# Re-dealing the first microseconds of a three-stage transformer kernel, with identity products on an idle tensor engine and an earlier load of the output weights

## The chip, the cores and the metric

The kernel runs on one core of a Trainium2 chip. The metric is the device time of one execution in microseconds (us); the smaller the better. The profile is one execution, whose span runs from the first to the last instruction.

## The reference, cut to what matters

Three residual blocks follow each other on `x` (16 batches of 64 tokens, 512 channels), with a context of 16 x 512 x 512:

```python
x = x + xattn(ctx_1024, layernorm(x), mask, ...)   # latents attend to the context and themselves
x = x + attn(layernorm(x), Wq, Wk, Wv, Wo, ...)    # differential self-attention over 64 tokens
x = x + ffn(layernorm(x), w_gate, w_up, w_down)    # SwiGLU, weights and activations in blockwise FP4

# inside xattn:
ln = _ln(latents, g_l, b_l)
q = ln @ w_q
k, v = split(concat([_ln(ctx), ln]) @ w_kv)
out = softmax(q k^T * scale, masked) @ v
return _ln(out @ w_out, g_o, b_o)
```

The change touches the first block only, and the rate at which FP4 weights for the third are prepared beside it.

## The kernel before, in words

Every product in high precision is made of three products of rounded halves: a matrix is split into a high part (a copy in fp32r, by `high`) and a low part (the rest, by `low`), and `Common.terms` (L114) runs high*high, high*low and low*high over the four chunks `k` of 128 channels. It is a generator that yields after each of the three terms.

**The opening** is `_latents` (L455). `load`, `weight` and `cw.load` issue DMAs on the one SyncE queue, in the order of the program: two tiles of x, four small vectors (`vec_rows`), four chunks of w_k, four of w_q, one of w_v. `raw` has nine buffers, so the other chunks of w_v wait until chunks of w_k are used up. `moments` (L493) makes the mean on VectorE and the inverse deviation on GpSimd (`tensor_scalar` L499, `pow` L500); `norm` (L502) normalises on VectorE; `turn` (L506) transposes a tile on TensorE and applies gain and bias on the way out of PSUM (ScalarE, L520, for tile 0; VectorE, L518, for tile 1); `upper` and `lower` split the result; `cw.turn` (L392) transposes the small vectors into `vec`, and its last line (L399) subtracts one bias from another on GpSimd. Then `heads` (L593) makes k and q of two tiles (`lk`, `lq`) and `values` (L634) makes v (`lv`), for four groups of two tiles. Between products, `then` runs the side work that `during(n, ...)` had filed under slot n: splits of other weights, moments of the next tiles, bias sums. In the first k of group 0, three of the four output chunks go together, term by term (`late = 3`, L607), because the low parts come late. PSUM has three banks for `cm.mm`/`cm.tr`, one for `ps_av`, and two pairs for `cm.two`. `take` (L598) empties a bank on ScalarE.

**The loop over 16 batches** is `cross_attention` (L729). The engines run what they are given in program order, each at its own pace. A batch has four `keys` (`pk`), four `values` (`pv`), two `scores`, and the transposes and weighing (`turn_both`, `turn_latents`, `finish`) of the batch before; every odd batch from 3 on has an output projection (`out_product`) too. `keys` is emptied by a VectorE multiply (L810), `values` by ScalarE (L823). ScalarE also splits the coming context (`cx.high`) and casts, and `weight_o` (L974) splits the output weights w_out: high on ScalarE, low on GpSimd. `load_o` (L970) loads one chunk of w_out; two buffers under tag "o" hold all four chunks in turn, so chunks 0 and 1 are loaded and split late in batch 0, chunks 2 and 3 loaded at its end and split early in batch 1.

**The quantiser** (L241) is a stream of 35 pieces of FP4 weights. `tick` moves every active piece by one step, and starts a piece every fourth tick. Step 1 loads (SyncE), step 3 is the block maximum on VectorE (L194 to L197), step 4 is on GpSimd, 5 and 6 on VectorE and ScalarE (L202 to L208), 7 on GpSimd, 8 and 9 on VectorE and ScalarE (L287 to L290), step 10 stores. Batch 0 has three ticks, each later batch ten.

Of the kernel before, what the change touches and what calls it, by code (L numbers as in the profile page):

```python
# [9 lines left out]
F32 = mybir.dt.float32  # L10
# [35 lines left out]
def f32(t):  # L46

    return t.bitcast(F32)


class Common:
# [62 lines left out]
    def terms(self, ps, parts, ks, start=True, stop=True):  # L114

        terms = [(0, 2), (0, 3), (1, 2)]
        n, last = 0, len(terms) * len(ks) - 1
        for i, j in terms:
            for k in ks:
                p = parts(k)  # L120
                self.nc.tensor.matmul(  # L121
                    ps, lhsT=p[i], rhs=p[j], start=start and n == 0, stop=stop and n == last
                )
                n += 1
            yield

    def split(self, hi, lo, src, by=None):

# [242 lines left out]
class CrossWeights:  # L371
# [20 lines left out]
    def turn(self):  # L392
        cm, nc = self.cm, self.cm.nc
        n = len(self.NAMES) * KC
        pt = cm.tr("vec_t")[:, :n]
        nc.tensor.transpose(pt, self.rows, cm.ident[:n, :n])
        nc.scalar.copy(self.vec, pt)

        nc.gpsimd.tensor_tensor(self.bl, self.bl, self.bx, ALU.subtract)  # L399


class SelfConstants:
# [52 lines left out]
def _latents(ctx, tc, cm, sc, i, cw, cx, sa):  # L455
# [13 lines left out]
    def load(*tiles):  # L469
        for p in tiles:  # L470
            nc.sync.dma_start(cm.x[p], i["x"][p * P : (p + 1) * P, :])
# [3 lines left out]
            raws[name, k] = pool.tile([P, D], F32, tag="raw", bufs=9, name=f"raw_{name}_{k}")  # L475
            nc.sync.dma_start(raws[name, k], source[name][k * P : (k + 1) * P, :])

    def high(name, w, k):
        nc.scalar.copy(w[0][:, k, :], raws[name, k])

    def low(name, w, k, by=None):
        by = by or (nc.vector, nc.gpsimd)[k % 2]
# [7 lines left out]

    def moments(p):  # L493
        st = cm.small.tile([P, 6], F32, tag="st", name=f"st_l_{p}")
        mv = mvs[p] = cm.small.tile([P, 2], F32, tag="mv", name=f"mv_l_{p}")
        nc.vector.bn_stats(st, cm.x[p])
        nc.vector.bn_aggr(mv, st)
        r = mv[:, 1:2]
        nc.gpsimd.tensor_scalar(r, r, 1.0 + LN_EPS, LN_EPS * LN_EPS, ALU.mult, ALU.add)  # L499
        nc.gpsimd.tensor_tensor(r, r, cm.mhalf[:, :1], ALU.pow)  # L500

    def norm(p):  # L502
        zs[p] = pool.tile([P, D], F32, tag="lz", bufs=2, name=f"lz_{p}")
        cm.normalize(zs[p], cm.x[p], f"l_{p}", mvs.pop(p))

    def turn(p):  # L506
        g, n = divmod(p, GT)
        if n == 0:
            lns[g] = tuple(
                pool.tile([P, KC, GT * P], F32R, tag=f"ln{h}", bufs=2, name=f"ln{h}_{g}") for h in "hl"  # L510
            )
        pt = cm.tr(f"lt_{p}")
        cm.transpose_chunks(pt, zs.pop(p), KC)
        ln = pool.tile([P, KC, P], F32, tag="ln", bufs=2, name=f"ln_{p}")
        for k in range(KC):
            src, scale, bias = pt[:, k * P : (k + 1) * P], cw.gl[:, k : k + 1], cw.bl[:, k : k + 1]
            if p == 1:
                nc.vector.tensor_scalar(ln[:, k, :], src, scale, bias, ALU.mult, ALU.add)  # L518
            else:
                nc.scalar.activation(ln[:, k, :], src, AF.Identity, bias=bias, scale=scale)  # L520
        rows[p] = ln

    def upper(*tiles):
        for p in tiles:
            g, n = divmod(p, GT)
            nc.vector.tensor_copy(lns[g][0][:, :, n * P : (n + 1) * P], rows[p])

    def lower(*tiles):
        for p in tiles:
            g, n = divmod(p, GT)  # L530
            hi, lo = (t[:, :, n * P : (n + 1) * P] for t in lns[g])
            nc.vector.tensor_tensor(lo, rows.pop(p), f32(hi), ALU.subtract)

    def bias(name, k):

# [57 lines left out]
    def heads(g, what, w, dst, scale, bias=None):  # L593

        hi, lo = lns[g]
        st = pool.tile([P, KC, GT * P], F32, tag=f"{what}st", name=f"{what}st_{g}")

        def take(m, ps):  # L598
            if bias is None:
                nc.scalar.copy(st[:, m, :], ps)  # L600
            else:
                nc.scalar.activation(
                    st[:, m, :], ps, AF.Identity, bias=bias[:, m : m + 1], scale=scale
                )


        late = 3 if (g, what) == (0, "k") else 0  # L607
        lag = 2 if (g, what) == (0, "q") else 0
        made, ready = [], []
        for m in range(KC):  # L610
            cols = slice(m * P, (m + 1) * P)
            ps = cm.mm(f"l{what}_{g}_{m}")[:, : GT * P]
            terms = cm.terms(
                ps,
                lambda k, cols=cols: (w[0][:, k, cols], w[1][:, k, cols], hi[:, k, :], lo[:, k, :]),
                range(KC),
            )
            made.append((m, ps, terms))
            if m < late - 1:
                continue  # L620
            for _ in range(3):
                for _, _, steps in made:
                    next(steps)
            for _ in made:
                then()
            ready += made
            made = []
            while len(ready) > lag:
                take(*ready.pop(0)[:2])
        for at, done, _ in ready:  # L630
            take(at, done)
        nc.sync.dma_start(dst[g], st)

    def values(g):  # L634
        hi, lo = lns[g]
        for n, p in enumerate(groups[g]):
# [9 lines left out]
            nc.scalar.copy(vst, ps)  # L646
            nc.sync.dma_start(sc.v[p], vst)

    load(0, 1)
    cw.load(pool)  # L650
    weight("k", *range(KC))
    weight("q", *range(KC))
    weight("v", 0)
    load(2, 3)
    moments(0)
    cw.turn()
    norm(0)
    moments(1)
    norm(1)
    high("k", w_k, 0)  # L660
    turn(0)
    turn(1)
    for k in range(1, KC):
        high("k", w_k, k)
    upper(0, 1)
    lower(0, 1)
    for k in range(KC):
        low("k", w_k, k, nc.vector)
    for k in range(KC):
        high("q", w_q, k)  # L670
    for k in range(KC):
        low("q", w_q, k)
    weight("v", 1, 2, 3)
    load(4, 5, 6, 7)
    sa.load_norm(pool)
# [3 lines left out]
    during(5, bias_sum, "q", cw.bq, S**-0.5)  # L679
    during(16, sa.turn_norm)  # L680
    for k in range(KC):
        during(1 + k, high, "v", w_v, k)
        during(2 + k, low, "v", w_v, k)
        during(7 + k, bias, "v", k)
    during(12, bias_sum, "v", cw.bv, 1.0)
    for n in range(2, NT):
# [42 lines left out]
def cross_attention(tc, cm, sc, i, cw, cx, w1, w2, att, quant):  # L729
# [238 lines left out]
    raw_o = {}  # L968

    def load_o(k):  # L970
        raw_o[k] = w1.tile([P, D], F32, tag="o", bufs=2, name=f"raw_wo_{k}")
        nc.sync.dma_start(raw_o[k], i["w_out"][k * P : (k + 1) * P, :])

    def weight_o(k):  # L974
# [18 lines left out]
    for b in range(B):  # L993

        def tick():
            if b:
                quant.tick()

        done = (b - 3) // 2 if b >= 3 and b % 2 else None
        last = b == B - 1  # L1000
        keys(b, 0)
        if last:
            att.load("Wq")
            att.load("Wk")
        cx.high(b + 1, 0)
        if b >= 4 and b % 2 == 0:
            out_moments((b - 4) // 2)
        tick()
        keys(b, 1)
        if b == 1:  # L1010
            weight_o(2)
            weight_o(3)
        cx.low(b + 1, 0)
        cx.high(b + 1, 1)
        tick()
        if b:
            turn_both(b - 1)
            turn_latents(b - 1)
        if done is not None:
            out_turn(done)  # L1020
        keys(b, 2)
        cx.fetch(b + 2, 0)
        cx.flat(b + 1)
        cx.low(b + 1, 1)
        cx.high(b + 1, 2)
        tick()
        if last:
            att.split("Wq", 0, 1)
        if b:
            finish(b - 1)  # L1030
        tick()
        if last:
            att.split("Wq", 2)
        scores(b, 0)
        softmax(b, 0)
        around(b + 1, 2, 3)
        keys(b, 3)
        cx.fetch(b + 2, 1)
        cx.low(b + 1, 2)
        cx.high(b + 1, 3)  # L1040
        tick()
        values(b, 0)
        cx.every(b + 1)
        cx.low(b + 1, 3)
        cx.stats(b + 2, 0)
        tick()
        if last:
            att.split("Wq", 3)
            att.load("Wv")
        if b == 0:  # L1050
            load_o(0)
            load_o(1)
        values(b, 1)
        begin(b + 1)
        cx.fetch(b + 2, 2)
        cx.stats(b + 2, 1)
        tick()
        if last:
            att.norm(0)
            att.split("Wk", 0, 1)  # L1060
        turn(b, 0, 0)
        turn(b, 0, 1)
        scores(b, 1)
        softmax(b, 1)
        around(b + 2, 0, 1)
        if done is not None:
            out_product(done)
        quant.tick()
        values(b, 2)
        cx.fetch(b + 2, 3)  # L1070
        cx.stats(b + 2, 2)
        quant.tick()
        if done is not None:
            out_norm(done)
            out_add(done)
        if b == 0:
            weight_o(0)
            weight_o(1)
            load_o(2)
            load_o(3)  # L1080
        if b == 2:
            att.sa.load()
        if b == 5:
            att.sa.work()
        if last:
            att.split("Wk", 2, 3)
            att.load("Wo")
            att.turn(0)
        values(b, 3)
        cx.stats(b + 2, 3)  # L1090
        cx.spread(b + 2)
        mask(b + 1)
        quant.tick()
        cx.load(b + 3)
    turn_both(B - 1)
# [635 lines left out]
```

## Time and profile before

| what | value |
|---|---|
| median of three runs | 912.67 us |
| lowest of three runs | 911.80 us |
| the profiled execution, time | 912.59 us |
| its span | 910.7 us |
| PE busy | 886.9 us (97%) |
| DVE, ACT, POOL busy | 682.1, 399.9, 330.5 us |
| chain that ended last, share of PE | 85% |

PE is TensorE's matmul side and PEld its weight loads; DVE is VectorE, ACT ScalarE, POOL GpSimd, SP SyncE, with a "q" for a sequencer. A timeline row is: start, duration, engine, line, operation, output<-inputs, shape, xcount, and in brackets the idle time ahead of it and what ended that. The chain that ended last is followed back from the last instruction to what released each step. A waits row is: engine, line and what it waited for, us in total, times, longest.

### The profile page before, as it was taken

Reading aid. Unit: us, or ns where it says so; the run is one execution under the profiler, and the core shown is the slowest. Engines: PE = TensorE matmul, PEld = TensorE weight load, DVE = VectorE, ACT = ScalarE, POOL = GpSimd, SP = SyncE. Lnnn points to the kernel's source line nnn. Section 1 sums busy time; section 2 is a strip of 40 time slices with the busy share of each in tenths; the row PEclk is TensorE's granted clock in tenths of the full one; section 3 lists DMA queues with packets and bytes.
Section 4 is the critical chain, followed back from the end, with each engine's and each line's share of the span. In section 5 each row is a group of like instructions: output and inputs, shape, how many; then the busy total and the mean of one; then the engine's idle time right before and its main releaser. Section 6 shows DMA issues by size and latency. Waiting matters only on the chain.

```text
span 910.7 us, 17129 instructions
## 1 busy us (share of the span) xinstructions
PE 886.9 (97%) x6550; PEld 733.2 (81%) x6550; DVE 682.1 (75%) x1394; ACT 399.9 (44%) x782; POOL 330.5 (36%) x376
## 2 busy tenths in 40 slices
PE   5999999999999999999999999999999999999998
PEld 5898777878787887888778877778777788888886
DVE  7545467878799787786997964586878797888875
ACT  4464344544545444445444545545454423322221
POOL 5255153326254353263443621547564330100000
PEclk9999999999999999999999999999999999999999
DMA  7464565554555445345544452140005530000000
GB/s 241 176 242 138 152 187 166 152 178 146 150 161 150 159 157 174 112 138 151 161 147 144 133 149 102 47 185 2 2 1 212 229 139 12 12 12 12 13 13 24
DMA packets 80235, 111.11 MB, mean 122 GB/s; under 512 B 33161, under 2 KB 38809, under 8 KB 78873
## 3 DMA queue, kind: packets, MB, share of 16 engines
q1 hardware_dynamic: 79992, 109.48, 37.5%
q8 instruction: 52, 0.85, 0.4%
q0 software_dynamic: 160, 0.52, 0.2%
q14 instruction: 31, 0.25, 0.1%
HBM read 84.26 MB, written 25.72 MB: 121 GB/s over the span
## 4 chain that ended last, share of the span: by engine, by line
PE 85%; DVE 7%; ACT 3%; DMA 2%; issue 1%; SPq 1%; POOL 1%; ACTq 0%; DVEq 0%; POOLq 0%
PE pk L121 18%; PE pv L121 18%; PE gu L121 13%; PE dn L121 7%; PE av L904 4%; PE sim L836 4%; PE prt L171 3%; PE po L121 3%; PE Wv L121 2%; PE lv L121 2%; PE wo L121 2%; PE lq L121 2%; PE lk L121 2%; DVE ex L1266 1%; PE ht L171 1%; DMA raw_wo<-in_w_out_dram 1%
## 5 line engine op out<-in xcount | busy, mean ns | idle before, releaser
L121 PE MATMUL pv<-xvh,x 128*128 128x512 f32 x512 | 133.1, 392 | 0.0
L121 PE MATMUL pk<-x,xkh 128*128 128x512 f32 x512 | 130.5, 397 | 0.3 <-DVE k L810 0.3
L121 PEld LDWEIGHTS pk<-x,xkh 128*128 128x128 f32 x512 | 93.7, 188 | 26.0 <-issue 4.0
L121 PEld LDWEIGHTS pv<-xvh,x 128*128 128x128 f32 x512 | 95.3, 188 | 23.3 <-issue 2.2
L810 DVE TENSOR_TENSOR k<-pk,row 128x512 f32<-128x512 f32 x64 | 43.6, 683 | 47.0 <-PE pk L121 46.8
L823 ACT ACTIVATE v<-pv,rs 128x512 f32<-128x512 f32 x64 | 43.9, 686 | 79.4 <-PE pv L121 79.3
L859 ACT ACTIVATE pr<-pr,least 128x576 f32<-128x576 f32 x64 | 49.2, 772 | 55.1 <-DVE least L855 54.8
L368 POOL TENSOR_TENSOR x<-raw,x 128x512 fp32r<-128x512 f32 x32 | 44.2, 1382 | 78.0 <-ACT x L362 71.6
L121 PE MATMUL pk<-x,xkl 128*128 128x512 f32 x256 | 68.7, 390 | 0.0
L121 PE MATMUL pv<-xvl,x 128*128 128x512 f32 x256 | 68.5, 389 | 0.0
L121 PE MATMUL gu<-uT,fx 128*128 128x512 f32 (+1 forms) x288 | 67.8, 378 | 0.0
L121 PE MATMUL gu<-gT,fx 128*128 128x512 f32 (+1 forms) x288 | 65.5, 375 | 0.0
L121 PEld LDWEIGHTS gu<-gT,fx 128*128 128x128 f32 x288 | 52.3, 188 | 7.6
L121 PEld LDWEIGHTS gu<-uT,fx 128*128 128x128 f32 x288 | 51.9, 188 | 7.2
L121 PEld LDWEIGHTS pk<-x,xkl 128*128 128x128 f32 x256 | 48.1, 188 | 10.4
L121 PEld LDWEIGHTS pv<-xvl,x 128*128 128x128 f32 x256 | 48.1, 188 | 10.2
L855 DVE CUSTOM_DVE_ANT_0 pr<-sim,mask 128x576 f32<-128x576 f32 x64 | 45.9, 754 | 6.2 <-PE sim L836 5.3
L321 DVE BATCH_NORM_STATS2 cst<-nat 128x6 f32<-128x512 f32 x64 | 42.8, 669 | 3.6 <-DMA nat<-in_ctx_dram 3.6
L121 PE MATMUL dn<-dT,hh 128*128 128x512 f32 x176 | 44.7, 393 | 0.6 <-ACT hh L129 0.6
L205 ACT ACTIVATE qe_h<-qe_h,mmagic 128x512 f32<-128x512 f32 (+1 forms) x24 | 16.5, 687 | 64.3 <-DVE qe_h L202 64.3
L871 ACT COPY prT<-prt 128x512 f32<-128x512 f32 x64 | 34.1, 585 | 18.1 <-PE prt L171 18.1
L904 PEld LDWEIGHTS av<-v,prT 128*64 128x64 f32 x1024 | 36.7, 138 | 5.6 <-issue 5.6
(302 smaller groups left out, 1963.0 us busy)
## 6 DMA issues: line engine op xcount, KB each, us to landing
nat<-in_ctx_dram SPq DMA_DIRECT2D x16, 1024.0 KB
raw<-in_ctxT_dram SPq DMA_DIRECT2D x64, 256.0 KB
d_d<-qhl_d SPq DMA_DIRECT2D x11, 512.0 KB
row<-rs_d SPq DMA_DIRECT2D x16, 256.0 KB
g_d<-qhl_g SPq DMA_DIRECT2D x8, 512.0 KB
u_d<-qhl_u SPq DMA_DIRECT2D x8, 512.0 KB
gT<-g_d SPq DMA_DIRECT2D x4, 1024.0 KB
uT<-u_d SPq DMA_DIRECT2D x4, 1024.0 KB
```

The lines of the kernel that those rows point to most:

```text
L121: self.nc.tensor.matmul(ps, lhsT=p[i], rhs=p[j], start=start and n == 0, stop=stop and n == last)
L171: self.nc.tensor.transpose(pt[:, c * P : (c + 1) * P], src[:, c * P : (c + 1) * P], self.ident)
L205: nc.scalar.activation(e, e, AF.Relu, bias=self.mmagic, scale=MAGIC)
L321: nc.vector.bn_stats(st, self.nat[b][:, j, :])
L368: by.tensor_tensor(lo, self.raw[:, c, :], f32(hi), ALU.subtract)
L810: nc.vector.tensor_tensor(k[:, S : S + N], ps, cx.row[b], ALU.mult)
L823: nc.scalar.mul(v, ps, cx.rs[b][:, t : t + 1])
L836: nc.tensor.matmul(pss[r][c * S : (c + 1) * S, h, :half], lhsT=queries[b % 2][rows, m, :], rhs=st["k"][m][rows, at : at + half], start=Tru ...
L855: nc.vector.tensor_tensor_reduce(two(pr), ps[:, :, :half], two(mask), -1.0, BIG, ALU.add, ALU.min, least)
L859: nc.scalar.activation(pr, pr, AF.Exp, bias=least, scale=-1.0, accum_out=st["tot"][:, t : t + 1])
L871: nc.scalar.copy(prT, pt.rearrange("p (j q) -> p j q", q=P))
L904: nc.tensor.matmul(st["av"][rows, 2 * a + r, :], lhsT=w[:, rows], rhs=v[:, at : at + S], start=(n == 0), stop=(n == len(pairs) - 1),)
```

## The change

It has three parts. The diff is cut to what the text speaks of.

**The opening.** The small vectors are queued behind the first two chunks of w_k. The x statistics are ordered anew, the short `tensor_scalar` of tiles 0 and 1 is moved from GpSimd to VectorE, and the bias subtraction (`less`) is moved behind both `pow`. Two chunks of w_k's high part go from ScalarE to VectorE, and the gain and bias of tile 1 are shared by both. All low parts of w_q are made on VectorE. The first k takes all four output chunks together, the fourth in the `ps_av` bank. `terms` yields after every matmul, so that the four chunks share each chunk of input. Splits of w_v are filed two slots later.

**Identity products.** `busy(n)` multiplies the identity by itself n times into a bank that nobody reads: nine times ahead of `cw.turn`, twice ahead of tile 1's transposes, four times behind them.

**Output weights and quantiser.** All four chunks of w_out have a buffer of their own and are loaded together in batch 0, behind `keys(0, 2)`; all are split at batch 0's end. Batch 0 has one tick in place of three, batch 1 nine in place of ten.

```diff
-            yield
+                yield
...
-        late = 3 if (g, what) == (0, "k") else 0
+        late = KC if (g, what) == (0, "k") else 0
...
+            ps = cm.ps_av.tile([P, D], F32, tag="av", name=name) if m == late - 1 else cm.mm(name)
...
+    idle = cm.two("idle")[:, 0, :P]
+    def busy(n):
+        for _ in range(n):
+            nc.tensor.matmul(idle, lhsT=cm.ident, rhs=cm.ident, start=True, stop=True)
     load(0, 1)
+    weight("k", 0, 1)
     cw.load(pool)
-    weight("k", *range(KC))
+    weight("k", 2, 3)
     weight("q", *range(KC))
     weight("v", 0)
     load(2, 3)
+    stats(0)
     moments(0)
-    cw.turn()
+    stats(1)
     norm(0)
     moments(1)
+    high("k", w_k, 0)
+    busy(9)
+    cw.turn()
+    cw.less()
+    turn(0)
     norm(1)
-    high("k", w_k, 0)
-    turn(0)
-    turn(1)
-    for k in range(1, KC):
-        high("k", w_k, k)
-    upper(0, 1)
+    busy(2)
+    turn(1, range(2))
+    high("k", w_k, 1)
+    busy(4)
+    high("k", w_k, 2, True)
+    high("k", w_k, 3, True)
+    upper(0)
+    weighed(1, range(2, KC), True)
+    upper(1)
     lower(0, 1)
...
-        low("q", w_q, k)
+        low("q", w_q, k, nc.vector)
...
-        during(1 + k, high, "v", w_v, k)
-        during(2 + k, low, "v", w_v, k)
+        during(3 + k, high, "v", w_v, k)
+        during((4, 4, 7, 7)[k], low, "v", w_v, k)
...
-        raw_o[k] = w1.tile([P, D], F32, tag="o", bufs=2, name=f"raw_wo_{k}")
+        pool, tag = ((w1, "o"), (w1, "o"), (w1, "oh"), (w2, "ol"))[k]
...
-        tick()
+        if b > 1:
+            tick()
         keys(b, 1)
-        if b == 1:
-            weight_o(2)
-            weight_o(3)
...
         cx.fetch(b + 2, 0)
+        if b == 0:
+            for k in range(KC):
+                load_o(k)
...
-        quant.tick()
+        tick()
...
         mask(b + 1)
+        if b == 0:
+            weight_o(2)
+            weight_o(3)
```

More of the change, by code (lines that the diff above doesn't have):

```diff
@@ L397, in turn, with less @@
         nc.scalar.copy(self.vec, pt)
-        nc.gpsimd.tensor_tensor(self.bl, self.bl, self.bx, ALU.subtract)
+    def less(self):
+        self.cm.nc.gpsimd.tensor_tensor(self.bl, self.bl, self.bx, ALU.subtract)
 class SelfConstants:
@@ L476, in weight, with high @@
             nc.sync.dma_start(raws[name, k], source[name][k * P : (k + 1) * P, :])
-    def high(name, w, k):
-        nc.scalar.copy(w[0][:, k, :], raws[name, k])
+    def high(name, w, k, vector=False):
+        copy = nc.vector.tensor_copy if vector else nc.scalar.copy
+        copy(w[0][:, k, :], raws[name, k])
     def low(name, w, k, by=None):
@@ L488, in split, with stats @@
             low(name, w, k)
+    def stats(p):
+        mvs[p, "st"] = cm.small.tile([P, 6], F32, tag="st", name=f"st_l_{p}")
+        nc.vector.bn_stats(mvs[p, "st"], cm.x[p])
     def moments(p):
-        st = cm.small.tile([P, 6], F32, tag="st", name=f"st_l_{p}")
+        if (p, "st") not in mvs:
+            stats(p)
         mv = mvs[p] = cm.small.tile([P, 2], F32, tag="mv", name=f"mv_l_{p}")
-        nc.vector.bn_stats(st, cm.x[p])
-        nc.vector.bn_aggr(mv, st)
+        nc.vector.bn_aggr(mv, mvs.pop((p, "st")))
         r = mv[:, 1:2]
-        nc.gpsimd.tensor_scalar(r, r, 1.0 + LN_EPS, LN_EPS * LN_EPS, ALU.mult, ALU.add)
+        by = nc.vector if p < GT else nc.gpsimd
+        by.tensor_scalar(r, r, 1.0 + LN_EPS, LN_EPS * LN_EPS, ALU.mult, ALU.add)
         nc.gpsimd.tensor_tensor(r, r, cm.mhalf[:, :1], ALU.pow)
@@ L504, in norm, with turn @@
         cm.normalize(zs[p], cm.x[p], f"l_{p}", mvs.pop(p))
-    def turn(p):
+    def turn(p, ks=range(KC)):
         g, n = divmod(p, GT)
@@ L513, in turn, with weighed @@
         cm.transpose_chunks(pt, zs.pop(p), KC)
-        ln = pool.tile([P, KC, P], F32, tag="ln", bufs=2, name=f"ln_{p}")
-        for k in range(KC):
+        rows[p] = pt, pool.tile([P, KC, P], F32, tag="ln", bufs=2, name=f"ln_{p}")
+        weighed(p, ks)
+    def weighed(p, ks, vector=False):
+        pt, ln = rows[p]
+        for k in ks:
             src, scale, bias = pt[:, k * P : (k + 1) * P], cw.gl[:, k : k + 1], cw.bl[:, k : k + 1]
-            if p == 1:
+            if vector:
                 nc.vector.tensor_scalar(ln[:, k, :], src, scale, bias, ALU.mult, ALU.add)
@@ L520, in turn @@
                 nc.scalar.activation(ln[:, k, :], src, AF.Identity, bias=bias, scale=scale)
-        rows[p] = ln
     def upper(*tiles):
@@ L525, in upper @@
             g, n = divmod(p, GT)
-            nc.vector.tensor_copy(lns[g][0][:, :, n * P : (n + 1) * P], rows[p])
+            nc.vector.tensor_copy(lns[g][0][:, :, n * P : (n + 1) * P], rows[p][1])
     def lower(*tiles):
@@ L531, in lower @@
             hi, lo = (t[:, :, n * P : (n + 1) * P] for t in lns[g])
-            nc.vector.tensor_tensor(lo, rows.pop(p), f32(hi), ALU.subtract)
+            nc.vector.tensor_tensor(lo, rows.pop(p)[1], f32(hi), ALU.subtract)
     def bias(name, k):
@@ L611, in heads @@
             cols = slice(m * P, (m + 1) * P)
-            ps = cm.mm(f"l{what}_{g}_{m}")[:, : GT * P]
+            name = f"l{what}_{g}_{m}"
+            ps = cm.ps_av.tile([P, D], F32, tag="av", name=name) if m == late - 1 else cm.mm(name)
+            ps = ps[:, : GT * P]
             terms = cm.terms(
@@ L620, in heads @@
                 continue
-            for _ in range(3):
-                for _, _, steps in made:
-                    next(steps)
+            for _ in range(3 if late else 1):
+                for _ in range(KC if late else 3 * KC):
+                    for _, _, steps in made:
+                        next(steps)
             for _ in made:
@@ L970, in load_o @@
     def load_o(k):
-        raw_o[k] = w1.tile([P, D], F32, tag="o", bufs=2, name=f"raw_wo_{k}")
+        pool, tag = ((w1, "o"), (w1, "o"), (w1, "oh"), (w2, "ol"))[k]
+        raw_o[k] = pool.tile([P, D], F32, tag=tag, bufs=2 if tag == "o" else 1, name=f"raw_wo_{k}")
         nc.sync.dma_start(raw_o[k], i["w_out"][k * P : (k + 1) * P, :])
@@ L1049, in cross_attention @@
             att.load("Wv")
-        if b == 0:
-            load_o(0)
-            load_o(1)
         values(b, 1)
@@ L1071, in cross_attention @@
         cx.stats(b + 2, 2)
-        quant.tick()
+        tick()
         if done is not None:
@@ L1078, in cross_attention @@
             weight_o(1)
-            load_o(2)
-            load_o(3)
         if b == 2:
```

## The prediction, written before the changed kernel was run

> **What bounds the kernel now.** I read the page's forty slices first: which engine is full, and where not.
>
> ```profile
> PE   5999999999999999999999999999999999999998
> PEclk9999999999999999999999999999999999999999
> ```
>
> TensorE is full from the second slice on; only the first slice (0 to 22.8 us) is open. So a change pays only where it takes idle or slow time out of TensorE's own row. Next, the timeline of the opening and one row of the same product later on:
>
> ```profile
> 5.10 0.26 PE L396 MATMUL vec_t<-ident,vec_rows 16*128 16x16 f32 x1 [5.10 <-DMA vec_rows<-in_g_x_dram]
> 8.24 1.12 PE L171 MATMUL lt<-ident,lz 128*128 128x128 f32 x4 [1.20 <-DVE lz L155]
> 11.31 7.60 POOL L483 TENSOR_TENSOR wql<-raw_q,wqh 128x512 fp32r<-128x512 f32 x2 [3.70 <-ACT wqh L479]
> 11.65 2.90 PE L121 MATMUL lk<-lnh,wkh 128*128 128x256 f32 x12 [2.29 <-DVE lnh L526]
> 14.35 2.37 PE L121 MATMUL lk<-lnl,wkh 128*128 128x256 f32 x12
> 16.56 1.60 PE L121 MATMUL lk<-lnh,wkl 128*128 128x256 f32 x12
> 17.79 4.16 DVE L541 SCALAR_TENSOR_TENSOR ws_bq<-raw_q,vec,ws_bq 128x512 f32<-128x512 f32 x3
> 26.58 0.63 PE L171 MATMUL lt<-ident,lz 128*128 128x128 f32 x4 [0.29 <-DVE lz L155]
> 27.84 0.63 PE L171 MATMUL lt<-ident,lz 128*128 128x128 f32 x4 [0.64 <-DVE lz L155]
> 28.23 1.18 PE L121 MATMUL lv<-wvh,lnh 128*128 128x512 f32 x4
> ...
> 33.79 0.64 PE L121 MATMUL lk<-lnh,wkh 128*128 128x256 f32 x4
> ```
>
> See three things. Dense work starts at 11.65. Its first twelve matmuls take 2.90 us, 242 ns each; the same ones from 33.79 on follow every 0.48 us by fours, 120 ns each. The first 24 last 4.91 us in place of 2.88, so about 2.0 us go to a slow start, which PEclk does not show. And around the transposes at 26.58 and 27.84 TensorE waits for VectorE.
>
> Then the batches: where the first `pk` of batches 1, 2 and 3 starts, the chain, and the waits of 90 to 160 us.
>
> ```profile
> 114.76 1.98 PE L121 MATMUL pk<-x,xkh 128*128 128x512 f32 x8
> ...
> 145.51 1.98 PE L121 MATMUL pk<-x,xkh 128*128 128x512 f32 x8
> ...
> 174.49 1.98 PE L121 MATMUL pk<-x,xkh 128*128 128x512 f32 x8
> ```
>
> ```profile
> 54.47 0.86 PE mean_k L574 x2
> ...
> 109.78 4.63 DMA raw_wo<-in_w_out_dram
> ...
> 117.75 4.81 DMA raw_wo<-in_w_out_dram
> ```
>
> ```profile
> DVE qm_g L194 <- DMA qw_g<-in_w_gate_dram: 7.3, 1, 7.3
> ACT woh L129 <- DMA raw_wo<-in_w_out_dram: 6.7, 3, 4.8
> ```
>
> Batch 1 takes 145.51 - 114.76 = 30.75 us, batch 2, with the same products, 28.98. So 1.77 us are lost in batch 1, and the chain passes there through w_out's loads: ScalarE stands 4.8 us at `woh`, behind it the casts and copies that `av` needs. Later even batches start 28.98 us apart, odd ones 32.2 to 32.4: with their output projection (2.72) and its transposes (0.44), 32.14 is due, so at most 0.3 is idle. There the kernel is at TensorE's pace.
>
> **The opening, cost by cost.** DMA: the loads land in queue order, 256 KB each 0.9 us (287 GB/s in 5 to 10 us); the chain has w_v's chunk landing at 12.59, which fits eleven of them. The small vectors, moved behind two chunks, are issued 0.9 us later (two issues of 0.43) and land at about 6.1 in place of 5.05; behind all their bytes, 6.9. Their copy on ScalarE ends at 6.7, `less` on GpSimd (0.29, now behind both `pow`) at about 7.2, so the gains of tile 0 (four of 0.375) run from 7.25 to 8.75, as now (7.15 to 8.65): nothing gained or lost. Tile 1: VectorE's `tensor_scalar` and the early statistics bring lz of tile 1 from 8.19 to 7.45. Two high parts move to VectorE (0.43 each, by the cast row of L526) and fit before 8.4. Then `upper(0)` 0.43, two gains 0.68, `upper(1)` 0.43: 10.45, where `lk` may start.
>
> `busy`: an fp32 product is two instructions (mean_k: 0.86 us for 512 columns), a quarter of it for 128 columns: 0.215 us warm, 0.43 cold. The identity is ready at 1.3, so nine of them lie in 1.4 to 5.3 under the wait for the vectors, at no cost. Two lie under the wait for lz. The last four stand directly ahead of `lk`: transposes end near 9.1, plus 0.86 (warm) or 1.72 (cold), 9.95 or 10.8. The start I take is 10.65, a gain of **1.0 us**.
>
> Is the array warm by then? The trace's row says that it took 11.65 to about 15.9, 4.2 us of unbroken work. The nine products last 3.9 us, then comes a break of 1 us, so by that row they may fall short; cold work from 6.2 on would end the ramp at 10.4, just at `lk`. The Trainium skill (TensorE: Matmul & The Clock Gate, Part 1) speaks more strongly against: the rate doubles after one busy window of about 3.4 us, and the windows run free of the kernel, so that a whole one is certain only after 6.8 us of work. Work from 6.2 on is then warm somewhere in 9.6 to 13.0. By the row, `lk` loses nothing; by the page, up to 2.4 us at half rate, 1.2 us of loss, on the mean some 0.5. I take 0.3 lost, for the early nine may count too.
>
> `lk` at full rate: 48 x 0.12 = 5.8 us. Low parts are in time: `lower` by 11.75, needed at 12.6; four low parts of w_k (0.62 each, as in 12.62 to 15.11) by 14.25, needed from 14.5. It ends at 16.8 with the loss; now at 19.4. The new order waits 0.2 at its end, because all four banks fill together and ScalarE empties the first only then. Gain beyond the start: 7.8 - 5.8 - 0.3 - 0.2 = **1.5 us**.
>
> `lq` keeps its length (6.8 us), if VectorE keeps up. It now makes all four low parts of w_q: 14.25 to 16.8, needed at 18. GpSimd's two took 3.8 us each while VectorE's bias steps (L541) took 1.39 each; the later rows of the same step are 0.74, so with GpSimd quiet the bias sum is ready at 16.8 + 0.5 + 3 x 0.74 = 19.5, needed at about 19.9. If that cover fails, `lq` waits 0.3. Then the statistics of tiles 2 and 3 follow, lz of tile 3 near 23.5, where TensorE is at 23.8. The two waits and loose ends between `lq` and `lv` (26.3 to 28.23, of which 0.9 is work) shrink by **1.0 us**. The splits of w_v, two slots later, end near 24.2; `lv` wants the low ones 0.9 us after its start at 24.7. Sum of the opening: 1.0 + 1.5 + 1.0 = **3.5 us**; bounds 1.0 (cold, vectors late) and 4.5. Behind it TensorE has no wait over a few tenths until 97, so I let it all carry through.
>
> **w_out.** Its four issues (0.43 each, 1.8 us) now stand on SP ahead of batch 1's `rs_d` stores, twelve small `k` loads, the row of scales and the mask. The row, landed near 112 now, is needed at 117.5; the mask, issued at 110.72, had one pair ahead of it already and moves by 0.9 us, with ScalarE wanting it at 116.5. So 2 to 4 us of cover; past it each us costs VectorE's L810 and so a bank. The chunks themselves land by 112.6 (1 MB at 228 GB/s, 110 to 120, behind the context that landed at 108.2); at today's 4.63 us a pair, 117.5. ScalarE reaches chunks 2 and 3 at about 116, so even then it waits 1.5 in place of 4.8, with no `pk` behind it before 121. The quantiser's first load moves to batch 0's last tick, and its block maximum from before `keys(1, 0)`'s emptying to behind `keys(1, 2)`: the 7.3 us wait goes, as three products (8.2 us) cover the 3 us load. Of the 1.77 us I take **1.4**; bounds -0.5 and 1.8.
>
> **The quantiser's shift.** Three ticks fewer: 150 in place of 153. Its last piece, begun at tick 136, ends at 145: the third tick of batch 15 before, the sixth now. So batch 15 gets L290, L202, L207 and L208 more on VectorE (0.68 + 0.42 + 1.38 = 2.5 us), beside idle stretches of 6.7 and 3.1 us there: 0 to 1.5, I take **0.2 lost**. In batches 2 to 14 each step falls one tick earlier. No row shows that placing; in 190 to 200 us VectorE is busy 9.7 of 10. But its 7.3 us stand in batch 1 held a `pk` up by only 0.5 us (weight load at 121.72), so three banks forgive much. Bounds -1.5 to +6 us over thirteen batches; I take 0, by that row.
>
> **Sum.** The profiled execution took 912.6 (a span of 910.7 and 1.9 around it), 0.1 below the median of the runs: no correction. 912.6 - 3.5 - 1.4 + 0.2 = **907.9 us**.
>
> **Rivals.** *The ramp stays* (18%): the vectors land late and the products don't warm the array before 13 us. For it: the page's free windows and the 1 us break; against it: the four us of mixed work ahead of `lk`. The opening gives 1.0 and the rest stays: 910.4. *w_out gives it back* (14%): SP's backlog (it stood 2.8 us in 104.7 to 107.5) makes row or mask late, so batch 1 keeps its loss: 909.3. *The quantiser's new place hurts* (12%), the one that ends slower: L207 and L208 now fall on L810 or the score reductions, and TensorE waits for a bank. From 0.38 us per batch (4.9 over thirteen) it eats everything; at 0.45 it gives 913.8. Against it: the 0.5 us above. *More than the sum* (6%): odd batches lose their 0.3 too, opening 4.5: 904.9. The forecast holds 50%, with its own range 906 to 909.8.
>
> **Range and chances.** The outer 2 in 10 are half of the better case and the worse part of the quantiser's and of the mishaps beyond it: 904.8 to 913.5. A measurement of this kernel can tell about 2% from no change, 18 us; no case comes near on the gain side: faster 0.01. Thirteen batches at 1.8 us each would be needed for slower: 0.03. Within 2%: 0.96.
>
> **What would show it.** First matmul of `lk` near 10.65, its rows at 120 ns; `lq` from 17, `lv` from 24.7; batch 1 within 0.5 us of 28.98; no wait of `woh` on its load over 2 us; even batches still 28.98 apart. It is wrong if `lk` rows keep 242 ns, if VectorE's bias step delays `lq`, if even batches grow, or if TensorE meets a new wait for a load between 25 and 100.

## The result, and the profile after

The changed kernel takes 915.82 us (median of seven runs, 914.09 to 916.38) against 912.67: the ratio is 1.0035, 95% interval 1.0025 to 1.0044. It is slower by about 3 us, well inside 2%, where 4.7 us of gain were forecast. The profiled execution's span is 914.0 us against 910.7. Lines of the program stand 31 lower from `cross_attention` on (L841 is the old L810).

The slices of the page show that the first one is now filled, and nothing else:

```profile
PE   8999999999999999999999999999999999999998
...
PEclk9999999999999999999999999999999999999999
```

Busy time is no gain here: the filling is the identity products, and a TensorE that waits two microseconds in thirty still shows a 9. So I set the two timelines side by side, stage by stage; the stages are cut at the first `pk` of each batch.

| stage | before, us | after, us | difference |
|---|---|---|---|
| start to the first `pk` | 89.41 | 87.72 | -1.69 |
| batch 0 | 25.35 | 26.55 | +1.20 |
| batch 1 | 30.75 | 28.98 | -1.77 |
| batches 2, 4, ... 14 | 202.87 | 210.24 | +7.37 |
| batches 3, 5, ... 13 | 194.11 | 192.96 | -1.15 |
| batch 15 to the end | 368.21 | 367.55 | -0.66 |
| span | 910.7 | 914.0 | +3.3 |

Even batches, which took 28.98 us each, now take 30.09, 30.37, 30.38, 29.39, 29.23, 30.38 and 30.40. Without the loss there the change would have won 4.1 us of span. The starts of the first `pk` of batches 2, 3, 4 and 5 in TensorE's timeline, after:

```profile
143.25 1.98 PE L121 MATMUL pk<-x,xkh 128*128 128x512 f32 x8
...
173.34 1.98 PE L121 MATMUL pk<-x,xkh 128*128 128x512 f32 x8
...
205.50 1.98 PE L121 MATMUL pk<-x,xkh 128*128 128x512 f32 x8
...
235.87 1.98 PE L121 MATMUL pk<-x,xkh 128*128 128x512 f32 x8
```

Where does TensorE stand in them? The waits of 262 to 282 us, in batch 6, after:

```profile
ACT qhl_g L288 <- issue: 8.6, 2, 6.7
...
PE av L935 <- ACT prl L920: 1.2, 1, 1.2
```

TensorE waits for `prl`, the last of ScalarE's three copies of the transposed probabilities, and ScalarE itself stood 6.7 us ahead of `qhl_g` (L288), the cast of the quantiser's step 8. "issue" means that the profile names no releaser, so the timelines have to. ScalarE in batch 6, after:

```profile
269.43 1.13 ACT L362 CAST x<-raw 128x512 fp32r<-128x512 f32 x2
277.22 0.62 ACT L288 CAST qhl_g<-qhl_g 128x512 fp32r<-128x512 f32 x1 [6.65 <-issue]
277.74 1.07 ACT L902 COPY prT<-prt 128x512 f32<-128x512 f32 x2
278.70 0.39 ACT L920 COPY prl<-prlt 128x256 f32<-128x256 f32 x1
```

And what the cast needed, in GpSimd's and VectorE's rows of the same stretch: the residual sum (L994), then step 7 of the piece (L210), then its transpose (L287).

```profile
270.07 1.63 POOL L994 TENSOR_TENSOR x<-x,oz 128x512 f32<-128x512 f32 x1
...
274.91 1.07 POOL L210 TENSOR_TENSOR qw_g<-qw_g,qs_g 128x512 f32<-128x512 f32 x1
```

```profile
276.44 0.70 DVE L287 STREAM_TRANSPOSE qhl_g<-qw_g 128x512 f32<-128x512 f32 x1
```

The transposes of the probabilities were done by 274.7, but their copies stood in ScalarE's queue behind a cast that wanted a chain through GpSimd. In the kernel before, no step of the quantiser on ScalarE stands in that place: steps 3 and 7 fall there, on VectorE and GpSimd. The last one ahead of it, `qe_u`, belongs to the last tick of batch 5 and is done before the casts; the copies follow the transposes at once:

```profile
272.14 0.73 ACT L205 ACTIVATE qe_u<-qe_u,mmagic 128x512 f32<-128x512 f32 x1 [2.44 <-DVE qe_u L202]
272.77 1.12 ACT L362 CAST x<-raw 128x512 fp32r<-128x512 f32 x2
274.72 1.08 ACT L871 COPY prT<-prt 128x512 f32<-128x512 f32 x2 [0.83 <-PE prt L171]
```

The opening after, in the timeline:

```profile
1.35 4.21 PE L668 MATMUL idle<-ident 128*128 128x128 f32 x18 [1.35 <-POOL mhalf L67]
...
8.21 1.06 PE L171 MATMUL lt<-ident,lz 128*128 128x128 f32 x4
9.06 1.65 PE L668 MATMUL idle<-ident 128*128 128x128 f32 x8
11.55 2.14 PE L121 MATMUL lk<-lnh,wkh 128*128 128x256 f32 x16 [0.84 <-DVE lnh L537]
13.53 2.08 PE L121 MATMUL lk<-lnl,wkh 128*128 128x256 f32 x16
...
21.24 1.02 PE L560 MATMUL bq<-ones,ws_bq 128*128 128x1 f32 x8 [0.48 <-DVE ws_bq L552]
...
26.48 1.18 PE L121 MATMUL lv<-wvh,lnh 128*128 128x512 f32 x4
```

`lk` starts hardly earlier (11.55 against 11.65), but at full rate (16 matmuls in 1.98 us, 124 ns each). `lv` starts 1.75 us earlier. The transposes and most of the products ahead of `lk` run slow here; more on that below.

### The profile page after: what moved, and what is told of

Its sections match the earlier page's. It is cut to its first block, busy times and chain, and to the rows that moved or that the text cites. A ratio compares the mean times of both kernels' runs of the same rounds, so it can differ in the third digit from the quotient of the medians.

```text
span 914.0 us, 17172 instructions
## 1 busy us (share of the span) xinstructions
PE 892.0 (98%) x6580; PEld 738.1 (81%) x6580; DVE 680.6 (74%) x1398; ACT 400.3 (44%) x782; POOL 319.5 (35%) x372
## 4 chain that ended last, share of the span: by engine, by line
PE 79%; DVE 9%; issue 5%; ACT 4%; POOL 2%; SPq 1%; DMA 1%; DVEq 0%; ACTq 0%; POOLq 0%
PE pv L121 16%; PE pk L121 14%; PE gu L121 13%; PE dn L121 7%; PE av L935 4%; PE sim L867 4%; PE po L121 3%; PE prt L171 2%; PE Wv L121 2%; PE lv L121 2%; PE wo L121 2%; PE lq L121 2%; PE lk L121 2%; DVE ex L1297 1%; PE ht L171 1%
## 5 line engine op out<-in xcount | busy, mean ns | idle before, releaser
L841 DVE TENSOR_TENSOR k<-pk,row 128x512 f32<-128x512 f32 x64 | 43.9, 686 | 61.8 <-PE pk L121 61.6
L368 POOL TENSOR_TENSOR x<-raw,x 128x512 fp32r<-128x512 f32 x32 | 41.7, 1304 | 70.7 <-ACT x L362 70.7
L205 ACT ACTIVATE qe_h<-qe_h,mmagic 128x512 f32<-128x512 f32 (+1 forms) x24 | 16.5, 687 | 64.4 <-DVE qe_h L202 64.4
L935 PE MATMUL av<-v,prT 128*64 128x64 f32 x1024 | 41.2, 224 | 0.0
```

Of the source, the lines that this page charges most:

```text
L205: nc.scalar.activation(e, e, AF.Relu, bias=self.mmagic, scale=MAGIC)
L368: by.tensor_tensor(lo, self.raw[:, c, :], f32(hi), ALU.subtract)
L841: nc.vector.tensor_tensor(k[:, S : S + N], ps, cx.row[b], ALU.mult)
L935: nc.tensor.matmul(st["av"][rows, 2 * a + r, :], lhsT=w[:, rows], rhs=v[:, at : at + S], start=(n == 0), stop=(n == len(pairs) - 1),)
```

## The experiments

My theory: the loss is a place in a queue. The quantiser's shift put a ScalarE step that hangs on GpSimd ahead of ScalarE's copies in even batches. Rivals: VectorE is fuller at the wrong time, whatever the order on ScalarE; the earlier opening disturbs what follows; the early output weights hold up a queue.

**opening_only**: the kernel before, with the new `_latents` and `terms`, and nothing of the rest.

> The kernel before with only the new opening (identity products included); output weights and quantiser as before. Theory (the loss is in the even batches and comes from the quantiser's new place): even batches 28.98 us apart as before, batch 1 keeps its 1.8 us loss, lv starts at 26.5, and the 1.7 us won up to the first pk are partly given back in batch 0, which waits for its k loads: span 909.0 to 910.5. Rival (the earlier start itself disturbs what follows): even batches grow here too, and the span is above 912.

Measured: span 909.9, median 912.07, ratio 1.0002 (0.9993 to 1.0011). Even batches stay at 28.98. First `pk` at 87.88, `lv` at 26.70, batch 0 25.59, batch 1 31.15. So the opening disturbs no even batch, and alone it moves the time by nothing that can be measured: of 1.5 us at the first `pk`, 0.6 are gone by batch 2.

**ticks_only**: the kernel before, with only the ticks moved.

```diff
-        tick()
+        if b > 1:
+            tick()
         keys(b, 1)
...
-        quant.tick()
+        tick()
         values(b, 2)
...
-        quant.tick()
+        tick()
```

> The kernel before with only the quantiser's start moved (one tick in batch 0, nine in batch 1), output weights loaded as before. Theory: even batches lose 0.3 to 1.4 us each, 7 us in all, odd ones win 0.2 each: span 914 to 917. Rival (it is the output weights or the opening): even batches stay 28.98, span 910 to 911.

Measured: span 914.6, median 916.35, ratio 1.0046 (1.0033 to 1.0059). Even batches take 30.09, 30.40, 30.35, 29.38, 29.24, 30.40 and 30.40, the changed kernel's own numbers. So the ticks alone make the whole loss. There was a surprise: batch 1 takes 28.98, although this kernel still loads w_out in pairs and ScalarE still waits for it, in the waits of 100 to 150 us:

```profile
ACT woh L129 <- DMA raw_wo<-in_w_out_dram: 4.6, 3, 2.6
```

**wout_only**: the kernel before, with only the four loads in batch 0 and the splits at its end.

> The kernel before with only the output weights loaded together in batch 0, ticks as before. Theory: batch 1 goes from 30.75 towards 28.98 and nothing else moves: span 909.0 to 909.7. Rival (the early loads hold up SyncE's queue): batch 0 or 1 grows, span 911 or more.

Measured: span 911.4, median 913.79, ratio 1.0019 (1.0012 to 1.0025); slower, against the theory. Batch 1 takes 31.50. No ScalarE wait for w_out is left in its waits of 100 to 150 us, but these are:

```profile
DVE qm_g L194 <- DMA qw_g<-in_w_gate_dram: 7.9, 1, 7.9
...
ACT qe_g L205 <- DVE qe_g L202: 6.9, 2, 6.7
...
PE av L904 <- ACT prl L889: 1.1, 1, 1.1
...
PE pk L121 <- DVE k L810: 0.9, 1, 0.9
```

So VectorE's wait for the quantiser's first load is enough for batch 1's loss: behind it TensorE stands 0.9 us at `pk`, for `keys`, and 1.1 us at `av`. The second is the main fault over again, for in batch 1 step 5 of the quantiser (L205) stands ahead of the copies on ScalarE, and it waits 6.7 us for VectorE. Moving w_out alone does not help; ahead of that load it makes it later still.

**tick_behind**: the changed kernel with two statements exchanged.

```diff
-        tick()
         if b:
             turn_both(b - 1)
             turn_latents(b - 1)
+        tick()
```

> The changed kernel with the second tick of each batch put behind the transposes of the batch before (turn_both, turn_latents) in place of ahead of them; the quantiser's phase stays. So on ScalarE the copies that av needs come ahead of the quantiser's cast of step 8. Theory (the cast waits for a late GpSimd and TensorE stands behind it): even batches back to 28.98, span 914.0 - 7.4 = 906.6, bounds 906 to 908. Rival (VectorE is fuller at the wrong time, whatever the order on ScalarE): even batches stay near 30.4, span 913 to 914.5.

Measured: span 906.7, median 909.38, ratio 0.9965 (0.9952 to 0.9977). All even batches take 28.98, all odd ones 32.16. The phase and the amount of VectorE work are those of the changed kernel; only the order on ScalarE is other, since `turn_both` and `turn_latents` give work to TensorE and ScalarE alone. The theory stands, and the rival of a full VectorE falls. The chain of work in 262 to 285 us is TensorE alone:

```profile
265.17 5.44 PE pk L121 x24
270.61 0.87 PE prt L171 x8
271.48 0.22 PE prlt L919 x2
271.70 2.75 PE pk L121 x12
274.45 2.48 PE av L935 x80
276.93 1.13 PE sim L867 x16
```

**one_tick_back and two_ticks_off**: the changed kernel with one tick more, and two fewer, in batch 1, so that another step of the quantiser stands in the disputed place. The first diff is that of `one_tick_back`, the second that of `two_ticks_off`.

```diff
-        if b > 1:
-            tick()
+        tick()
         keys(b, 1)
```

```diff
         cx.high(b + 1, 1)
-        tick()
+        if b > 1:
+            tick()
...
         cx.high(b + 1, 2)
-        tick()
+        if b > 1:
+            tick()
```

> The changed kernel with batch 1's first tick given back: ten ticks in batch 1, every later step one place earlier in its batch than in the kernel after. Theory (what counts is whether a ScalarE step of the quantiser that hangs on a GpSimd step stands ahead of the transposes' copies in even batches): step 5 (L205) now stands there, behind step 4 on a late GpSimd, so even batches stay slow, 29.5 to 30.5, span 911 to 914.5. Rival (it is the mere count or lateness of the ticks): about one third of the way back, even batches near 29.8 all over or less, and no step 5 in the chain.

Measured: span 932.7, median 935.26, ratio 1.0242 (1.0202 to 1.0281). Even batches 29.64, 34.00, 35.18, 32.79, 31.08, 32.55 and 32.50. The direction was forecast, the size was not: some 0.7 to 6.2 us a batch in place of 0.5 to 1.5. Its chain in batch 4 has the theory's two ends, the residual sum and step 5 (L205) ahead of the copies; between them it runs through step 7 on GpSimd (L210) and VectorE's own queue (L287, L290), and not through step 4:

```profile
207.72 1.29 POOL x L994
...
210.65 1.03 POOL qw_u L210
...
214.98 1.49 DVE qe_u L202
...
216.56 0.72 ACT qe_u L205
217.28 0.96 ACT prT L902 x2
218.24 0.28 ACT prl L920
...
218.56 3.50 PE av L935 x67
```

In 143 to 580 us TensorE waits for the last of the copies in all seven even batches:

```profile
PE av L935 <- ACT prl L920: 17.6, 7, 3.4
```

That is 17.6 of the 24.9 us that these batches lose against 28.98 each. The granted clock can account for most of the rest: its mean of 0.993 over 932.7 us is about 6.5 us, by my estimate.

> The changed kernel with two more ticks taken from batch 1 (seven in it). Theory: in even batches steps 2, 6 and 10 now stand ahead of the transposes' copies, none of which is on ScalarE, so even batches go to 28.98 to 29.2 and the span to 906.5 to 909 although the quantiser begins still later; step 8 stands there in odd batches, where GpSimd has no residual sum to finish, 32.16 to 32.6. Rival (later is worse): even batches at 30.4 or above, span 914 or more.

Measured: span 908.4, median 911.15, ratio 0.9983 (0.9969 to 0.9997). All even batches take 28.98, with the quantiser later than in any other kernel, so lateness is not what costs. Odd ones take up to 32.85, 0.25 more than forecast. In batch 3, 0.7 us over 32.16, TensorE's weight loads wait 0.3 us for `prl` behind step 8, which VectorE's transpose (L287) makes late here and not GpSimd; most of the rest goes at `po`, where ScalarE's copy `v` stands behind another step 8.

**tb_no_busy and tb_busy_long**: `tick_behind` without the identity products, and with ten in place of the last four.

```diff
-    busy(9)
...
-    busy(2)
...
-    busy(4)
```

```diff
-    busy(4)
+    busy(10)
```

The question comes from `tick_behind`'s own opening, in which `lk` was slow in spite of the products:

```profile
7.86 0.60 PE L171 MATMUL lt<-ident,lz 128*128 128x128 f32 x4
8.29 1.06 PE L668 MATMUL idle<-ident 128*128 128x128 f32 x8
11.52 3.60 PE L121 MATMUL lk<-lnh,wkh 128*128 128x256 f32 x16 [2.17 <-ACT wqh L482]
```

The transposes run at full rate (0.60; 1.12 before), the last four products end at 9.35, TensorE stands 2.2 us, and `lk` starts at 215 ns a matmul (16 in the 3.44 us to its next row). In the changed kernel the transposes were slow (1.06), the products ended at 10.7, and `lk` was fast. The opening of both is the same code: the nine early products took 4.21 us in the changed kernel's trace and 3.78 in this one.

> The kernel of tick_behind without the fifteen identity products. Theory (the products warm the array, but often too early: it stands still for 2 us ahead of lk and is slow again): lk's first 24 matmuls take about 4.9 us as before the change, lk to lq 7.5 to 7.8 us, and the span is 0 to 1.5 us above 906.7, so most of the opening's gain remains without them. Rival (the products carry the opening): the span is 2 us or more above 906.7.

Measured: span 907.4, median 909.16, ratio 0.9964 (0.9950 to 0.9978). `lk` to `lq` takes 8.1 us, more than the 7.5 to 7.8 forecast; `lk` starts at 11.20, so `lq` starts only 0.25 later than in `tick_behind`. Next to `tick_behind`, whose products ended too early, they are worth nothing that these times show. That does not hold for every execution: in the traces of the changed kernel, `one_tick_back` and `two_ticks_off`, with the same opening, `lk` to `lq` takes 6.09 us and the first `pk` starts at 87.7, against 88.66 here.

> The kernel of tick_behind with ten identity products in place of four ahead of the first lk, so that TensorE has work until lk can start. Theory: with the pause closed, every lk matmul takes 120 ns, lk to lq 6.1 us in place of 7.5, span 905.0 to 906.0; if the products run slow they reach past 11.5 and cost up to 1.5 us of it. Rival (the pause is not what slows lk): first lk matmuls near 225 ns again, span 906.7 or more.

Measured: span 906.2, median 907.91, ratio 0.9952 (0.9938 to 0.9966). The pause is closed, and the rate holds:

```profile
7.90 2.40 PE L668 MATMUL idle<-ident 128*128 128x128 f32 x20
10.74 2.14 PE L121 MATMUL lk<-lnh,wkh 128*128 128x256 f32 x16 [0.45 <-DVE lnh L537]
```

`lk` to `lq` takes 6.09 us. First `pk` at 86.86, 1.5 earlier than in `tick_behind`; but the span wins only 0.5, since batch 0 takes 26.29. The intervals of the three overlap: the ranking rests on the stage times of one trace each, not on the medians.

**keys_first and queries_keys_first**: `tb_busy_long` with another order of batch 0's loads on SyncE's queue, for batch 0 now stands at its first scores.

```diff
+    around(0, 0, 1)
     begin(0)
     mask(0)
-    around(0, 0, 1, 2, 3)
+    around(0, 2, 3)
```

In `queries_keys_first` the four loads stand inside `begin` instead, behind the queries:

```diff
-        mu = w1.tile([P, N], U8, tag="mu", name=f"mu_{b}")
-        nc.sync.dma_start(mu, i["mask"][b : b + 1, :].to_broadcast([P, N]))
         with nc.allow_non_contiguous_dma(reason="the latents of a batch"):
             nc.sync.dma_start(queries[e], sc.q[g][:, :, mine])
+        if b == 0:
+            around(0, 0, 1)
+        mu = w1.tile([P, N], U8, tag="mu", name=f"mu_{b}")
+        nc.sync.dma_start(mu, i["mask"][b : b + 1, :].to_broadcast([P, N]))
...
-    around(0, 0, 1, 2, 3)
+    around(0, 2, 3)
```

> The kernel of tb_busy_long, with the four loads that batch 0's first scores need put ahead of its mask, queries and latents on SyncE's queue. Theory (with an earlier opening, batch 0's scores stand for a k load that comes behind five others): batch 0 goes from 26.3 to 25.35, span 905.0 to 905.5. Rival (the load itself lands late, wherever it is queued): batch 0 stays at 26.3, span 906.2.

Measured: span 906.8, median 907.64, ratio 0.9950 (0.9937 to 0.9962). A miss: batch 0 takes 26.94. The scores now wait for the queries (tile `mask`), which I had put last:

```profile
97.26 1.20 PE L867 MATMUL sim<-k,mask 64*64 64x288 f32 x16 [1.51 <-DMA mask<-q_d]
```

> The kernel of tb_busy_long, with the queries and then the four k loads of batch 0's first scores ahead of its mask and latents on SyncE's queue. Theory (batch 0's scores stand for the last of five loads on one queue; keys_first only exchanged which one was last): the five are issued by 91.3, landed by 94.5, and batch 0 takes 25.35, span 905.0 to 905.5. Rival (these loads land late wherever they stand, because something else holds the queue or the DMA engines): batch 0 stays at 26 or more, span 906 or more.

Measured: span 904.5, median 906.61, ratio 0.9945 (0.9931 to 0.9959). Batch 0 takes 25.36, and the scores start without a wait:

```profile
95.09 1.20 PE L869 MATMUL sim<-k,mask 64*64 64x288 f32 x16
```

This is the best version: it beats both kernels, though its interval overlaps those of `tb_busy_long` and `keys_first`. It has the change's quantiser start, one exchange of order, a closed pause and another order of five loads.

**old_opening_behind**: `ticks_only` with `tick_behind`'s exchange; the old opening and w_out in pairs.

> The kernel before, with its own opening and the output weights loaded in pairs as before; only the late quantiser, and the second tick behind the transposes. Theory (batch 1 was cured by the late quantiser and not by the output weights; the rest is TensorE's pace): batch 1 and all even batches 28.98, odd ones 32.16, first pk at 89.4, span 907.5 to 908.0. Rival (the early output weights matter): batch 1 near 30.75, span 909 or more.

Measured: span 908.1, median 909.78, ratio 0.9970 (0.9959 to 0.9982). Batch 1 and all even batches take 28.98, odd ones 32.16, first `pk` at 89.58. Three fewer ticks and one exchange of statements make up 2.6 of the 6.2 us of span that the best version wins; the early output weights add nothing to batch 1.

## Why the prediction was wrong, point by point

**The quantiser's shift is the step that failed**: "In batches 2 to 14 each step falls one tick earlier. No row shows that placing ... I take 0, by that row." It cost 7.4 us in the even batches and won 1.2 in the odd ones, a net 6.2 against bounds of -1.5 to +6. The row I priced it by was the wrong engine's. VectorE's 7.3 us in batch 1 showed how much delay TensorE's three banks forgive in `keys`. What the shift moved was also a ScalarE instruction, and behind it on that engine stood the copies that `av` needs, which have one `keys` product (2.75 us) of time and take 1.4 of it themselves. The rows for it were there: batch 1 of the kernel before, where TensorE stands 1.0 us at `av` behind ScalarE's queue (the wait for w_out, then L205, then the copies), the odd batches' residual sum on GpSimd, and which step of a piece falls between `keys(b, 1)` and `turn_both` in every second batch, which can be counted from the ticks. I named what is queued behind for SP's loads, and not for the thirteen batches of ScalarE. The rival that ended slower (913.8) had the right stage and nearly the right price, but the wrong mechanism: L207 and L208 on VectorE and a missing bank. `tick_behind` leaves those where they are and loses nothing.

**w_out.** "Of the 1.77 us I take 1.4." Batch 1 did win 1.77 in the changed kernel, but not from w_out: `ticks_only` wins all of it with the pairs, `wout_only` none of it. The chain named the w_out loads because ScalarE's wait for them was the last one on it; VectorE's wait for the quantiser's load lay beside it, and moving the ticks shortened the wait for w_out too (its longest from 4.8 to 2.6). In `wout_only` L205 took w_out's place in holding ScalarE up. I saw both waits and added them up under the part that the chain named. What it does to SyncE's queue showed only where the quantiser's load came behind it.

**The opening.** 3.5 us forecast, 1.75 measured at `lv`, 1.69 at the first `pk`. Its terms: the start of `lk`, forecast +1.0, was +0.1, since slow transposes (1.06 against 0.60) and the gains behind them moved `upper(1)` to 10.97. With fast ones it was +0.9 in `tb_busy_long` and +0.6 in `opening_only`, but again +0.1 in `tick_behind`, where VectorE stands 1.31 us for a late chunk of w_k: the start is not sure from one execution to the next. The rate, forecast +1.5, was +1.7 here, and +0.3 in `tick_behind`, so that in the changed kernel's trace it came by luck: because the last products ran slow, they ended at 10.7 and left a pause of 0.84 us. There I had mis-seen the danger. By the row and by the page I asked whether the array would be warm in time (the 6.8 us was my estimate from the page's window). Its free windows fit the traces: the same nine products from 1.35 us on took 4.21 us in one trace and 3.72 in another (`queries_keys_first`). But what happened in two executions is that it was warm early and slow again after some 2 us of standing. My 242 ns a matmul counted the row's tail in: by their starts the first twelve are 225 ns apart. `lq`, forecast 0, lost 0.8: VectorE's bias steps took 1.08 each and not 0.74, beside GpSimd's split of w_v (19.00 to 20.55; in `tick_behind`, where the split starts at 20.42, they took 0.78), so the bias sum came at 21.1, not 19.5. The end, forecast +1.0, was +0.7.

**"So I let it all carry through"** failed too: 1.2 us went in batch 0, where the first scores wait for a `k` load (issued at 93.48, landed at 97.13):

```profile
97.18 1.18 PE L867 MATMUL sim<-k,mask 64*64 64x288 f32 x10 [0.50 <-DMA k<-k_d]
```

From the first of these scores to the next `pk` it is 2.32 us, against 1.13 before. I had checked that TensorE has no wait there at present, not how little slack there was. `queries_keys_first` gives it back.

**What held**: batch 1 within 0.5 us of 28.98 (by luck, since the part that I credited wins nothing alone), no wait of `woh` over 2 us, batch 15 at no loss, and the size of all this against 2%. Among the signs of error I had written "if even batches grow".

## What to carry to other kernels

Moving a stream of small side jobs by one step is not a change of its amount but of its place in every queue: list, for each engine, which instruction of it lands directly ahead of which copy that the busy engine needs, and what its own input hangs on. Price it by the slack of the consumer behind it on that engine, not by the most forgiving wait in the profile. A chain of waits names the last of several waits that run side by side, so a part of a change is credited with a stall only if undoing that part alone brings it back.

## What the runs showed of the hardware that I had not expected

TensorE can fall back to the slow rate after a pause of 2 us. In `opening_only` it stood 1.96 us ahead of `lk`, in `tick_behind` 2.17 us, both after a stretch of broken work. The columns of the last two rows are: us, busy PE, PEld, DVE, ACT, POOL, granted clock, DMA share, GB/s; all are of `opening_only`.

```profile
7.99 1.06 PE L668 MATMUL idle<-ident 128*128 128x128 f32 x8
11.00 2.83 PE L121 MATMUL lk<-lnh,wkh 128*128 128x256 f32 x16 [1.96 <-DVE lnh L537]
```

```profile
11.00:12.00 1.00, 1.00 (x8) 1.00 (x9) 1.00 (x3) 0.71 (x2) 0.00 (x0) 1.00 0.87 258
13.00:15.00 2.00, 2.00 (x11) 2.00 (x11) 2.00 (x5) 0.55 (x1) 0.00 (x0) 0.50 0.66 230
```

There `lk` starts at full rate, eight matmuls in the first us, and the clock falls about a us later, with TensorE at work; in `tick_behind` it is 0.50 in 11.5 to 14.5 us, from `lk`'s start on. Part 1 of "TensorE: Matmul & The Clock Gate" in the Trainium skill speaks of at least one idle window of about 3.4 us. In neither trace did TensorE stand that long, so for this kernel the rule is too mild; whether a window that is idle in part is enough, no run here shows. The profile's clock does not show the slow start of the kernel before, where it says 1.000.

In `one_tick_back`, after a pause of 3.3 us, the `av` matmuls came to take 1.07 us for sixteen in place of 0.64, and the stretch of 220 to 240 us was granted 0.94.

```profile
220.00:240.00 20.00, 20.00 (x144) 15.79 (x141) 15.33 (x36) 9.25 (x18) 5.87 (x7) 0.94 0.51 148
```

So its stalls paid twice, but the fall-back is not the whole surplus over the forecast: another execution of that kernel, with a mean granted clock of 0.998, still had a span of 927.0 us, where 911 to 914.5 had been expected. The longer waits at `av` are the other part, and why they grew so much stays open.
